# Graph network stack on one core: LSTMs over single nodes with output gates of two chunks by seven products, and GpSimd multiplying gates and writing last states

## The chip, the core and the metric

The kernel runs on one core of a Trainium2 chip. A core has five engines that run side by side, each with its own queue of instructions in a fixed order: TensorE for matrix products (PE in the profile, its weight loads PEld), VectorE (DVE), ScalarE (ACT), GpSimd (POOL) and SyncE (SP), which here issues the transfers. They wait for one another by semaphores. Matrix products land in PSUM, in banks of 512 float32 values in each of 128 partitions; the other data lie in SBUF.

The metric is the device time of one execution in microseconds (us), lower is better. Three runs of the kernel before took 2249.4, 2252.04 and 2255.14 us, median 2252.04. What a measurement of this kernel can tell from no change is about 0.3%, some 6.8 us.

## What is computed

The input is x[128, 64, 256], 128 graphs of 64 nodes with 256 features, and one adjacency matrix. Four layers run one after the other, each as `x = x + layer(relu(layernorm(x)))`. The change lies in the third, `_L2_gnn_ref`, cut here to its second half:

```python
for p in range(1, MAX_SKIP + 1):          # p = 1..4
    nw = Tv // p                          # 64 // p windows of p nodes
    wins = h[:, :nw * p, :].reshape(Bv * nw, p, Hd)
    last = _lstm_last(Wih[p - 1], Whh[p - 1], bih[p - 1], bhh[p - 1], wins)
    idx = jnp.arange(nw) * p + (p - 1)
    h = h.at[:, idx, :].set(last.reshape(Bv, nw, Hd))
# one LSTM step, state (h, c), zero at the start
g = x_t @ Wih.T + h @ Whh.T + bias
i, f, gg, o = jnp.split(g, 4, axis=-1)
c = sigmoid(f) * c + sigmoid(i) * tanh(gg)
h = sigmoid(o) * tanh(c)
```

For p = 1 a window is a single node. There is one step from a zero state, so the forget gate and Whh drop out: `h = sigmoid(o) * tanh(sigmoid(i) * tanh(g))`.

## The kernel before

All work is in float32. The 128 graphs are held as four groups q of 32 graphs, in four large tiles `big`; `nodes(q)` gives a group as H[128 partitions, 2 feature halves, 64 nodes, 32 graphs]. Sixteen tiles X0 to X15 of [128, 4, 256] hold x itself. In layer 2 each of them is written out to a buffer in device memory (`xs<-X` in the profile), after which its place serves the LSTM as scratch: `flat[i]` is X(i) seen as [128, 1024].

`windows` runs p = 1 to 4. For p = 1 there are 16 chunks of 16 nodes (four per group), worked in eight pairs; a chunk has 16 x 32 = 512 columns. `lstm(p, t, ch, Ws)` does one step of one chunk. A gate has 256 outputs, two blocks of 128. A plain product of a gate needs four matmuls of 512 columns: two output blocks by two feature halves. The kernel mostly uses a scheme of seven products of half the width (Strassen's, in the variant with few additions): the 32 graphs are cut in two halves of 16, and sums of data quarters are multiplied with sums of weight quarters.

- The data sums T0 to T3 are the four parts of a tile `ls_tx` (pool of two buffers). VectorE makes them per chunk with three subtractions: one of 128x512 (T0 and T1 together), then two of 128x256 (T2, then T3). Both inputs of these lie in SBUF.
- The weight sums S1 to S4 are made once per p by `weights(p)`, which also loads the weights: even p into tiles `ls_w`, odd p into X4 to X7 (Wih) and X0 to X3 (Whh). It is called for p + 1 before the second pair of p; SyncE and VectorE have the transfers and sums in their fixed order.
- `product(m, bank, first)` issues product m for two gates at once, each into one half of a bank. The order is 1, 6, 7, 5, 2, 4, 3, into four banks a, b, f and d; products 2, 4 and 3 add on top of banks a, f and d.
- ScalarE copies product 1 to Z (`ls_z`). VectorE adds: Z = Z + product 6; U = Z + product 7; V11 = U + product 5; V10 = Z + (7 + 4); V01 = Z + (5 + 3). The sum of products 1 and 2 is read from its bank. So product 2 has to wait for the copy of Z, product 4 for the addition U and product 3 for the addition V11, because they write into the bank that is read there.
- ScalarE applies sigmoid or tanh with the bias, quarter by quarter.

For p = 1 a chunk calls `gates` twice. The first call makes the input gate i and the candidate g, 14 matmuls of 256 columns. The second makes the output gate o on its own, by plain products, 4 matmuls of 512 columns; the results come out of PSUM by two ACTIVATEs with no addition. VectorE then multiplies i and g to c (128x1024, `X<-ls_g`), ScalarE takes tanh of c, and VectorE writes the last state into H with two multiplications of 128x512 (`last_state`, `big<-ls_g` in the profile). A float32 matmul is recorded as two MATMULs.

The order on each engine is fixed when the kernel is built, by a scheduler that follows the order of the calls and its own costs. In the profile nearly every instruction has line 799, since a helper records them all, so groups are told apart by the names of their tiles.

Of the kernel before, what the change touches and what calls it, by code (L numbers as in the profile page):

```python
# [8 lines left out]
F32 = mybir.dt.float32  # L9
# [903 lines left out]
class Fast:  # L913
# [28 lines left out]
    def act(self, out, a, f, **kw):  # L942
        return self.nc.scalar.activation(out, a, f, **kw)
# [500 lines left out]
P = 128  # L1444
NB = 16
# [20 lines left out]
class Kernel:  # L1466
# [35 lines left out]
    def begin(self):  # L1502
        nc, o, io = self.nc, self.o, self.io
        self.ident = self.c("ident", P, P)
        make_identity(nc, self.ident)
        self.ones = self.c("ones", P, P)
        nc.vector.memset(self.ones[:], 1.0)
        self.A, self.AT = self.c("A", N, N), self.c("AT", N, N)
        nc.sync.dma_start(self.A[:], io["adj"])
        nc.sync.dma_start(self.AT[:], io["adj_t"])  # L1510
        self.X = []
        for i in range(NB):
            self.X.append(self.c(f"X{i}", P, TPB, D))
        self.load_x(0)

    def load_x(self, i):
# [687 lines left out]
    def windows(self):  # L2204

        nc, o, io = self.nc, self.o, self.io
        cx, (w, wq, gp, tp, zp, psum, pst) = self.stage([("lsw", 1), ("lswq", 1), ("lsg", 2), ("lst", 2), ("lsz", 2),  # L2210
                                                         ("lsps", 7), ("lstps", 1)], "tile")
        with cx:
            bias = w.tile([P, 4, 8], F32, name="ls_b")
            bh = w.tile([P, 4, 8], F32, name="ls_bh")
            with nc.allow_non_contiguous_dma("a few values"):
                nc.sync.dma_start(bias[:], io["L2_gnn_bih"].rearrange("q (k p) -> p q k", p=P))
                nc.sync.dma_start(bh[:], io["L2_gnn_bhh"].rearrange("q (k p) -> p q k", p=P))
            o.add(bias[:], bias[:], bh[:])
            flat = [x[:].rearrange("p t d -> p (t d)") for x in self.X]
            self.c_, self.h_, self.th_ = Ring(flat[12:15]), Ring(flat[8:10]), Ring(flat[10:12])  # L2220
            self.u_ = Ring([flat[15][:, 0:512], flat[15][:, 512:1024]])
            self.lp = gp, tp, zp, psum, bias

            def load(ap, n, x):

                if x is None:
                    return ([wq.tile([P, 4 * D], F32, name=f"ls_w{n}{kc}")[:] for kc in range(2)]
                            + [wq.tile([P, 2 * D], F32, name=f"ls_s{n}{i}")[:] for i in range(3)])
                return [flat[x], flat[x + 1], flat[x + 2][:, 0:512], flat[x + 2][:, 512:1024], flat[x + 3][:, 0:512],
                        flat[x + 3][:, 512:1024]]  # L2230

            def weights(p):

                out = []
                for n, m in enumerate(("Wih", "Whh") if p > 1 else ("Wih",)):
                    t = load(None, n, None if p % 2 == 0 else 4 - 4 * n)
                    ap = io[f"L2_gnn_{m}_t"][p - 1]
                    for kc in range(2):
                        nc.sync.dma_start(t[kc], ap[kc * P:(kc + 1) * P, :])
                    A = [[t[kc].rearrange("p (x k m) -> p x k m", k=2, m=P)[:, :, k, :] for kc in range(2)]  # L2240
                         for k in range(2)]
                    S1, S2, S4 = (y.rearrange("p (x m) -> p x m", m=P) for y in t[2:5])
                    o.add(S1, A[1][0], A[1][1])
                    o.sub(S2, S1, A[0][0])
                    o.sub(S4, A[0][1], S2)
                    S3 = t[5].rearrange("p (x m) -> p x m", m=P) if len(t) > 5 else A[1][0]
                    o.sub(S3, A[0][0], A[1][0])
                    out.append({1: A[0][0], 2: A[0][1], 3: S4, 4: A[1][1], 5: S1, 6: S2, 7: S3,
                                "A": A})
                return out  # L2250

            ready = weights(1)
            for p in range(1, 5):
                Ws = ready
                nw = N // p
                parts = -(-nw // 16)
                chunks = []
                for q in range(NG):
                    w0 = 0
                    for k in range(parts):  # L2260
                        w1 = w0 + (nw - w0) // (parts - k)
                        chunks.append((q, w0, w1))
                        w0 = w1
                for n in range(0, len(chunks), 2):
                    if n == 2 and p < 4:
                        ready = weights(p + 1)
                    if n == 2 and p == 4:
                        self.fetch(0, 8)
                        for i in range(8):
                            self.back(i, pst, "pt")  # L2270
                    two = [dict(q=q, w0=w0, w1=w1) for q, w0, w1 in chunks[n:n + 2]]
                    two[-1]["last"] = p == 4 and n + 2 >= len(chunks)
                    for t in range(p):
                        for ch in two:
                            self.lstm(p, t, ch, Ws)
            self.fetch(8, NB)
# [17 lines left out]
    def lstm(self, p, t, ch, Ws):  # L2294
# [25 lines left out]

        def gates(xs, fs):
            G = gp.tile([P, 2, 1024], F32, name="ls_g")
            if p == 1 and len(xs) == 1:
                for k in range(2):
                    ps = psum.tile([P, BT], F32, name="ps")
                    for kc in range(2):
                        self.mm(ps[:, 0:2 * W].rearrange("p (w b) -> p w b", b=32), Ws[0]["A"][k][kc][:, xs[0], :],
                                node(kc), kc == 0, kc == 1)
                    self.act(G[:, 0, 2 * W * k:2 * W * (k + 1)].rearrange("p (h w b) -> p h w b", h=2, b=16),
                             ps[:, 0:2 * W].rearrange("p (w h b) -> p h w b", h=2, b=16), fs[0],  # L2330
                             bias=bias[:, p - 1, 2 * xs[0] + k:2 * xs[0] + k + 1])
                return G
            n = len(xs)
            V = G[:, 0:n, 0:4 * W].rearrange("p x (k h w) -> p x k h w", k=2, h=2)
            banks = {}

            def product(m, bank, first):
                if first:
                    banks[bank] = psum.tile([P, 2, 256], F32, name="ps")
                for i, x in enumerate(xs):  # L2340
                    for j, (A, Bm) in enumerate(parts):
                        out = banks[bank][:, i, 0:W]
                        if len(Bm[m].shape) == 3:
# [24 lines left out]
            return G  # L2368
# [24 lines left out]
        else:  # L2393
            self.last_state(H, at, W, s(G, 0), s(G, 1))

    def last_state(self, H, at, W, *factors):

        for k in range(2):
            y = H[:, k, at, :].rearrange("p w (h b) -> p h w b", h=2)
            self.o.mul(y, *(x[:, 2 * W * k:2 * W * (k + 1)].rearrange("p (h w b) -> p h w b", h=2, b=16) for x in factors))  # L2400

# [470 lines left out]
```

## Time and profile before

| what | value |
|---|---|
| median of three runs | 2252.04 us (2249.4 to 2255.14) |
| profiled execution, its time | 2254.63 us |
| its span in the profile | 2252.8 us |
| granted TensorE clock, mean | 0.997 |
| p = 1 (677.6 to 830.1 us): PE / DVE / ACT / POOL busy | 151.65 / 118.26 / 92.90 / 0.00 us of 152.5 |
| p = 2 and a part of 3 (830.1 to 1005 us): PE / DVE / ACT busy | 174.90 / 121.99 / 78.29 us of 174.9 |

Groups within p = 1, from the groups of instructions by shape in that stretch (count, mean of one): ACT ls_z copies of 128x512 x16, 600 ns; DVE additions of 128x512 from PSUM x80, 682 to 687 ns; DVE products c of 128x1024 x15, 1226 ns; DVE last states of 128x512 x30, 688 ns; ACT tanh of 128x1024 x15, 1050 ns.

A span is what the profiler saw of one execution; 2254.63 - 2252.8 = 1.83 us lie around it. Times in the trace count from the start of the span. A line of the timeline gives the start, the time from the first start to the last end of a run of like instructions, the engine, the operation, output <- inputs, shapes and count; in brackets stands how long the engine was idle before and who ended that.

### The profile page before, as it was taken

What the parts mean: (1) busy time and instruction counts of PE and PEld (TensorE: products, weight loads), DVE (VectorE), ACT (ScalarE), POOL (GpSimd) and SP (SyncE); (2) the same over time, 40 slices, a digit from 0 to 9 for tenths busy, and PEclk for the clock granted to TensorE, in tenths of its full rate; (3) what the DMA queues carried; (4) which work ended last, traced back from release to release, by engine and by line L of the source; (5) the groups of instructions that cost most, each with busy time, mean ns of one, the idle gap of its engine ahead of it and who ended that gap; (6) DMA issues with size and microseconds to landing.
All of it is one profiled execution on the core that took longest, in us unless ns stands there. A gap on an engine that the chain in (4) does not pass through costs nothing.

```text
span 2252.8 us, 33666 instructions
## 1 busy us (share of the span) xinstructions
PE 2214.0 (98%) x12617; PEld 1614.5 (72%) x12617; DVE 1610.7 (71%) x4073; ACT 1143.7 (51%) x2500; POOL 7.2 (0%) x33
## 2 busy tenths in 40 slices
PE   7999998999999999999999999999999999999999
PEld 4554444667777778888999999888888555555654
DVE  8777576888538776676767676756955787777767
ACT  5667864665435663444444443433634664444431
POOL 1000000000000000000000000000000000000000
PEclk9999999999999999999999999999999999999999
DMA  6000220122000000000100001000001000000001
GB/s 181 1 1 10 75 54 27 59 93 47 1 24 5 1 19 1 1 1 1 38 1 1 1 1 60 16 1 1 13 1 51 29 1 15 15 20 20 15 24 48
DMA packets 61070, 54.88 MB, mean 24 GB/s; under 512 B 15203, under 2 KB 58724, under 8 KB 60900
## 3 DMA queue, kind: packets, MB, share of 16 engines
q1 hardware_dynamic: 60900, 52.66, 7.6%
q8 instruction: 101, 1.65, 0.3%
q14 instruction: 69, 0.57, 0.1%
HBM read 35.86 MB, written 16.78 MB: 23 GB/s over the span
## 4 chain that ended last, share of the span: by engine, by line
PE 77%; DVE 4%; ACT 1%; issue 1%; DMA 0%; ACTq 0%; DVEq 0%
PE ps L799 70%; PE pt L799 4%; PE acc L799 3%; DVE sm_m L799 1%; DVE X L799 1%; PE pe L799 1%; DVE aw L799 1%; DVE XV L799 0%; ACT ls_g L799 0%; ACT h L799 0%; DMA ls_w<-in_L_gnn_Wih_t_dram 0%; DVE lin_s L799 0%; DVE lin_p L799 0%; DVE hT L799 0%; DVE n_st L799 0%
## 5 line engine op out<-in xcount | busy, mean ns | idle before, releaser
L799 ACT ACTIVATE ls_g<-ls_g,ls_b 128x512 f32<-128x512 f32 (+4 forms) x472 | 243.3, 565 | 146.8 <-DVE ls_g L799 144.7
L799 ACT ACTIVATE ls_g<-ps,ls_b 128x256 f32<-128x256 f32 (+3 forms) x268 | 115.6, 470 | 335.9 <-PE ps L799 332.8
L799 PE MATMUL ps<-z,w 128*128 128x512 f32 x512 | 257.1, 624 | 0.0
L799 PE MATMUL ps<-big,X 128*128 128x176 f32 (+3 forms) x848 | 212.7, 366 | 0.1
L799 DVE TENSOR_TENSOR ls_g<-ls_z,ps 128x512 f32<-128x512 f32 (+5 forms) x258 | 147.3, 577 | 90.7 <-PE ps L799 89.0
L799 PE MATMUL ps<-ls_tx,X 128*128 128x160 f32 (+2 forms) x960 | 206.9, 326 | 1.4 <-DVE ls_tx L799 0.9
L799 PE MATMUL ps<-X,X 128*128 128x160 f32 (+1 forms) x896 | 199.1, 306 | 0.0
L799 PE MATMUL ps<-X,ls_w 128*128 128x256 f32 x640 | 190.5, 379 | 0.1
L799 PEld LDWEIGHTS ps<-ls_tx,X 128*128 128x128 f32 x960 | 161.7, 190 | 16.3 <-DVE X L799 4.7
L799 DVE TENSOR_TENSOR aw<-at,ed_OST 128x1024 f32<-128x1024 f32 x128 | 150.3, 1220 | 28.7 <-PE ps L799 28.5
L799 ACT ACTIVATE r<-ps 128x512 f32<-128x512 f32 x256 | 129.4, 621 | 74.6 <-PE ps L799 74.5
L799 PEld LDWEIGHTS ps<-big,X 128*128 128x128 f32 x848 | 145.9, 190 | 29.7 <-issue 19.4
L799 DVE TENSOR_TENSOR X<-ls_g 128x1024 f32<-128x1024 f32 (+2 forms) x108 | 117.5, 1088 | 50.6 <-ACT ls_g L799 50.6
L799 PEld LDWEIGHTS ps<-X,X 128*128 128x128 f32 x896 | 148.4, 190 | 0.0
L799 PE MATMUL ps<-X,ls_s 128*128 128x256 f32 x480 | 142.7, 379 | 0.0
L799 PEld LDWEIGHTS ps<-z,w 128*128 128x128 f32 x512 | 87.5, 191 | 67.6 <-issue 60.4
L799 PE MATMUL ps<-ls_tx,ls_s 128*128 128x256 f32 x464 | 134.7, 379 | 0.0
L799 PEld LDWEIGHTS ps<-X,ls_w 128*128 128x128 f32 x640 | 121.3, 190 | 16.8 <-DVE X L799 0.5
L799 PE MATMUL ps<-ls_tx,ls_w 128*128 128x256 f32 x464 | 133.3, 380 | 0.0
L799 PE MATMUL ps<-big,ls_w 128*128 128x256 f32 x464 | 131.9, 379 | 0.7 <-ACT ls_z L799 0.7
L799 PE MATMUL ps<-aw,ed_ODT 128*32 128x512 f32 x1024 | 122.0, 593 | 0.1
L799 PE MATMUL ps<-ed_S,Q 64*128 64x512 f32 x512 | 121.0, 604 | 0.9 <-DVE X L799 0.9
(560 smaller groups left out, 3938.7 us busy)
## 6 DMA issues: line engine op xcount, KB each, us to landing
X<-in_x_dram SPq DMA_DIRECT2D x32, 512.0 KB
xs<-X SPq DMA_DIRECT2D x16, 512.0 KB
X<-xs SPq DMA_DIRECT2D x16, 512.0 KB
out_dram<-X SPq DMA_DIRECT2D x31, 256.0 KB
X<-in_L_gnn_Wih_t_dram SPq DMA_DIRECT2D x4, 512.0 KB
ls_w<-in_L_gnn_Wih_t_dram SPq DMA_DIRECT2D x4, 512.0 KB
ls_w<-in_L_gnn_Whh_t_dram SPq DMA_DIRECT2D x4, 512.0 KB
w<-in_L_gnn_W_t_dram SPq DMA_DIRECT2D x2, 512.0 KB
```

The source lines that it names most:

```text
L799: i = method(*a, **kw)
```

## The change

1. X0 to X15 become eight tiles of two, `X2`, so that two neighbours are one tile of [128, 2, 1024]. Each X is a view of half a tile.
2. For p = 1 a new function `single` replaces `lstm`, for a pair of chunks A and B at a time. It calls `gates` three times: i and g of A; i and g of B; then o of A and o of B together. Each call has seven products of two, 14 matmuls of 256 columns. The plain product is gone.
3. The gates land in a ring of five tiles, X2 numbers 4, 5, 6, 0, 1, in place of the pool `ls_g`. c is written over the gate i, and its tanh over the gate g.
4. The product c (128x1024) and the last states (two of 128x512 per chunk) are issued on GpSimd.
5. The data sums of both chunks are held until the output gates of the pair are done, in the same two buffers of `ls_tx`.

```diff
+        self.X2 = [self.c(f"X{i}", P, 2, TPB, D) for i in range(0, NB, 2)]
+        self.X = [x[:, i] for x in self.X2 for i in range(2)]
...
+            self.g_ = Ring([self.X2[i][:].rearrange("p x t d -> p x (t d)") for i in (4, 5, 6, 0, 1)])
...
                     two[-1]["last"] = p == 4 and n + 2 >= len(chunks)
+                    if p == 1:
+                        self.single(two, Ws[0])
+                        continue
...
         def gates(xs, fs):
             G = gp.tile([P, 2, 1024], F32, name="ls_g")
-            if p == 1 and len(xs) == 1:
-                for k in range(2):
-                    ps = psum.tile([P, BT], F32, name="ps")
-                    for kc in range(2):
-                        self.mm(ps[:, 0:2 * W].rearrange("p (w b) -> p w b", b=32), Ws[0]["A"][k][kc][:, xs[0], :],
-                                node(kc), kc == 0, kc == 1)
-                    self.act(G[:, 0, 2 * W * k:2 * W * (k + 1)].rearrange("p (h w b) -> p h w b", h=2, b=16),
-                             ps[:, 0:2 * W].rearrange("p (w h b) -> p h w b", h=2, b=16), fs[0],
-                             bias=bias[:, p - 1, 2 * xs[0] + k:2 * xs[0] + k + 1])
-                return G
...
+    def single(self, two, A):
+        nc, o = self.nc, self.o
+        gp, tp, zp, psum, bias = self.lp
+        I, F, G, O = range(4)
+        data = []
+        for ch in two:
+            H, at = self.nodes(ch["q"]), slice(ch["w0"], ch["w1"])
+            T = tp.tile([P, 4, 256], F32, name="ls_tx")[:].rearrange("p n (w b) -> p n w b", b=16)
+            o.sub(T[:, 0:2], H[:, :, at, 16:32], H[:, 0, at, :].rearrange("p w (h b) -> p h w b", h=2))
+            o.sub(T[:, 2], H[:, 1, at, 16:32], T[:, 0])
+            o.sub(T[:, 3], H[:, 1, at, 0:16], T[:, 2])
+            data.append({1: H[:, 0, at, 0:16], 2: H[:, 1, at, 0:16], 3: H[:, 1, at, 16:32],
+                         5: T[:, 0], 7: T[:, 1], 6: T[:, 2], 4: T[:, 3]})
+        def gates(pairs, act):
+            tile = self.g_.next()
+            V = tile.rearrange("p x (k h w) -> p x k h w", k=2, h=2)
...
+            a = product(1, "a", True)
+            self.act(Z, a, AF.Copy)
+            o.add(Z, Z, product(6, "b", True))
+            o.add(U, Z, product(7, "f", True))
+            o.add(V[:, :, 1, 1], U, product(5, "d", True))
+            a = product(2, "a", False)
+            act(V[:, :, 0, 0], a, 0)
+            o.add(V[:, :, 1, 0], Z, product(4, "f", False))
+            act(V[:, :, 1], V[:, :, 1], 1)
+            o.add(V[:, :, 0, 1], Z, product(3, "d", False))
+            act(V[:, :, 0, 1], V[:, :, 0, 1], 0)
+            return tile
...
+        def together(out, a, k):
+            self.act(out, a, AF.Sigmoid, bias=bias[:, 0, 2 * O + k:2 * O + k + 1])
+        cells = []
+        for b in data:
+            V = gates(((I, b), (G, b)), apart)
+            nc.gpsimd.tensor_tensor(V[:, 0], V[:, 0], V[:, 1], op=ALU.mult)
+            self.act(V[:, 1], V[:, 0], AF.Tanh)
+            cells.append(V)
+        V = gates([(O, b) for b in data], together)
+        for i, ch in enumerate(two):
+            self.last_state(self.nodes(ch["q"]), slice(ch["w0"], ch["w1"]), 256, V[:, i], cells[i][:, 1], engine=nc.gpsimd)
```

`apart` issues one ACTIVATE per gate (sigmoid for i, tanh for g), `together` one for both chunks. `last_state` takes the engine as an argument, VectorE where none is given.

More of the change, by code (lines that the diff above doesn't have):

```diff
@@ L1510, in begin @@
         nc.sync.dma_start(self.AT[:], io["adj_t"])
-        self.X = []
-        for i in range(NB):
-            self.X.append(self.c(f"X{i}", P, TPB, D))
+        self.X2 = [self.c(f"X{i}", P, 2, TPB, D) for i in range(0, NB, 2)]
+        self.X = [x[:, i] for x in self.X2 for i in range(2)]
         self.load_x(0)
@@ L2218, in windows @@
             o.add(bias[:], bias[:], bh[:])
-            flat = [x[:].rearrange("p t d -> p (t d)") for x in self.X]
+            flat = [x.rearrange("p t d -> p (t d)") for x in self.X]
+            self.g_ = Ring([self.X2[i][:].rearrange("p x t d -> p x (t d)") for i in (4, 5, 6, 0, 1)])
             self.c_, self.h_, self.th_ = Ring(flat[12:15]), Ring(flat[8:10]), Ring(flat[10:12])
@@ L2247, in weights @@
                     o.sub(S3, A[0][0], A[1][0])
-                    out.append({1: A[0][0], 2: A[0][1], 3: S4, 4: A[1][1], 5: S1, 6: S2, 7: S3,
-                                "A": A})
+                    out.append({1: A[0][0], 2: A[0][1], 3: S4, 4: A[1][1], 5: S1, 6: S2, 7: S3})
                 return out
@@ L2394, in lstm, with product, apart @@
             self.last_state(H, at, W, s(G, 0), s(G, 1))
-    def last_state(self, H, at, W, *factors):
+    def single(self, two, A):
[14 more added lines that the diff above has]
+            V = tile.rearrange("p x (k h w) -> p x k h w", k=2, h=2)
+            banks = {}
+            def product(m, bank, first):
+                if first:
+                    banks[bank] = psum.tile([P, 2, 256], F32, name="ps")
+                for i, (x, b) in enumerate(pairs):
+                    nc.tensor.matmul(banks[bank][:, i, :].rearrange("p (w b) -> p w b", b=16), A[m][:, x, :], b[m],
+                                     start=first and i == 0, stop=i == 1, skip_group_check=True)
+                return banks[bank][:]
+            Z = zp.tile([P, 2, 256], F32, name="ls_z")[:]
+            U = self.u_.next().rearrange("p (x w) -> p x w", x=2)
+            a = product(1, "a", True)
[10 more added lines that the diff above has]
+            return tile
+        def apart(out, a, k):
+            for i, (x, f) in enumerate(((I, AF.Sigmoid), (G, AF.Tanh))):
+                self.act(out[:, i], a[:, i], f, bias=bias[:, 0, 2 * x + k:2 * x + k + 1])
+        def together(out, a, k):
[9 more added lines that the diff above has]
+            self.last_state(self.nodes(ch["q"]), slice(ch["w0"], ch["w1"]), 256, V[:, i], cells[i][:, 1], engine=nc.gpsimd)
@@ L2398, in last_state @@
+    def last_state(self, H, at, W, *factors, engine=None):
         for k in range(2):
             y = H[:, k, at, :].rearrange("p w (h b) -> p h w b", h=2)
-            self.o.mul(y, *(x[:, 2 * W * k:2 * W * (k + 1)].rearrange("p (h w b) -> p h w b", h=2, b=16) for x in factors))
+            (engine or self.nc.vector).tensor_tensor(y, *(x[:, 2 * W * k:2 * W * (k + 1)].rearrange("p (h w b) -> p h w b", h=2, b=16) for x in factors), op=ALU.mult)
     def edges(self, w, pool, psum):
```

## The prediction

> **What bounds the kernel now.** First the page's busy times: TensorE is busy nearly always, VectorE three quarters of the time, GpSimd practically never.
>
> ```profile
> span 2252.8 us, 33666 instructions
> PE 2214.0 (98%) x12617; PEld 1614.5 (72%) x12617; DVE 1610.7 (71%) x4073; ACT 1143.7 (51%) x2500; POOL 7.2 (0%) x33
> ```
>
> A busy PE need not be the limit, so I read the chain of waits from 677 to 835 us, the stage that is changed. From the first data sums on it is TensorE alone:
>
> ```profile
> 677.85 1.64 DVE ls_tx L799 x3
> 679.53 155.48 PE ps L799 x592
> ```
>
> The busy times by stretch say the same: 151.65 us of matmuls in 152.50. Whatever makes TensorE wait here costs its full length.
>
> ```profile
> 677.60:830.10 152.50, 151.65 (x577) 109.13 (x577) 118.26 (x187) 92.90 (x160) 0.00 (x0) 1.00 0.00 1
> ```
>
> The timeline gives the pace. The same step of two neighbouring chunks:
>
> ```profile
> 727.15 2.75 PE L799 MATMUL ps<-ls_tx,X 128*128 128x256 f32 x12
> 736.63 2.75 PE L799 MATMUL ps<-ls_tx,X 128*128 128x256 f32 x12
> ```
>
> A chunk takes 736.63 - 727.15 = 9.48 us. It holds 14 matmuls of 256 columns and 4 of 512, 22 units of 256, so a unit costs 9.48 / 22 = 0.431 us. A product for two gates (two units) is 0.862 us.
>
> Two things that the change brings hardly occur before, and the timeline shows one trace of each. GpSimd, at the start of the program, beside VectorE:
>
> ```profile
> 40.20 1.49 POOL L1807 TENSOR_SCALAR big<-big 128x512 f32<-128x512 f32 x1
> 40.22 0.66 DVE L799 SCALAR_TENSOR_TENSOR f_x<-f_v,f_uk,f_x 64x57 f32<-64x57 f32 x1
> 41.77 1.26 POOL L1808 TENSOR_TENSOR big<-big 128x512 f32<-128x512 f32 x1
> 41.98 1.06 DVE L799 SCALAR_TENSOR_TENSOR f_h_t<-f_h_r,f_x,f_h_s 64x1 f32<-64x1 f32 x1
> ```
>
> and the same VectorE instruction a little earlier, alone:
>
> ```profile
> 37.58 0.21 DVE L799 SCALAR_TENSOR_TENSOR f_h_t<-f_h_r,f_x,f_h_s 64x1 f32<-64x1 f32 x1
> ```
>
> GpSimd needs 1.26 us for 128x512. An instruction of VectorE that reads two operands from SBUF stood still meanwhile, 1.06 us in place of 0.21, until 43.04, just when GpSimd was done (43.03). And the weights: Whh of p = 3 was loaded long ahead, Wih at the end of p = 1:
>
> ```profile
> 500.13 0.35 SPq L2239 DMA_DIRECT2D X<-in_L_gnn_Whh_t_dram  x1
> 829.87 1.19 SPq L2239 DMA_DIRECT2D X<-in_L_gnn_Wih_t_dram  x2
> 835.26 0.69 DVE L799 TENSOR_TENSOR X<-X,X 128x512 f32<-128x512 f32 x1 [0.20 <-DMA X<-in_L_gnn_Wih_t_dram]
> ```
>
> Two loads of 512 KB take 835.26 - 829.87 = 5.4 us from issue until a sum can use them.
>
> **The change, part by part.**
>
> *Products.* A pair had 44 units and has 42: 8 pairs x 2 x 0.431 = **-6.9 us**. That is all that can be gained, since TensorE has only some 0.85 us of idle time in the stage.
>
> *ScalarE and VectorE.* Per pair the second gate call needs a Z copy (0.60) more and five VectorE additions (back to back 0.60 each, as 732.53, 733.13, 733.73 in the trace). VectorE loses two products c (1.23) and four last states (0.65). Per pair of 18.1 us it has 15 additions and the data sums 2 x (0.60 + 0.36 + 0.36): 11.6 us. The sums of busy times fit; the order in the queues decides.
>
> *GpSimd.* Six multiplications per pair: two of 128x1024, four of 128x512 with strided output. The row says 1.26 for 512; for 1024 I take 2.45, a little under twice 1.26 (2.52). Low bound: VectorE's own 1.23 and 0.65. High bound: the longest row of that size, 1.49, and as no row writes strided, 0.3 more, as much as lies between 1.26 and 1.49 and a little: 1.8. I take the row of the same operation. Sum 4.9 + 5.04 = 9.9 us, room enough, but ScalarE's tanh of c waits in its queue for the first two, and behind it the sigmoids and the next Z copy.
>
> *A steady pair.* I set the queues in the order of the built kernel side by side by hand, with the spacings of the rows (VectorE 0.60 and 0.36; ScalarE 0.42, 0.62, 1.05; 0.20 after a matmul, as the ls_z copy; 0.05 after others). Time 0 is product 1 of chunk A.
>
> - The data sums of A may only be made when the previous output call has finished product 4, as both buffers are held. T2 of A is ready at 0.90, product 6's turn is 0.86: stall 0.09.
> - The output gates' ACTIVATEs end at 2.32; GpSimd's four last states run from 2.46 on.
> - VectorE's T2 of B comes at 2.51 and waits for the first one, to 3.72; ends 4.08. Addition Z to 4.68. T3 of B waits for the second (4.08 to 5.34), ends 5.70. Addition U, queued behind, ends 6.30. Product 4's turn is 4.39, but it overwrites what U reads: it starts at 6.35. Stall 1.96.
> - In the output call ScalarE is late: tanh of A (to 13.88, since c comes at 12.73), six gate ACTIVATEs to 16.84, Z copy to 17.42, additions Z and U to 18.72; product 4's turn is 18.41. Stall 0.36.
>
> Together 42 x 0.431 + 0.09 + 1.96 + 0.36 = 20.5 us per pair against 18.95. The first pair has no seam behind it, 19.2. Stage: 19.2 + 7 x 20.5 = 162.7 against 152.5: **+10.2 us**. If the sums need not wait for GpSimd the same table gives 18.7 per pair, 150.1, -2.4 us.
>
> *Weight sums of p = 2.* Eight sums of two SBUF inputs fall into the first two pairs, beside the first products c. One or none behind a multiplication: 0 to 2.45; I take **+1**.
>
> *The end of p = 1.* The ring's last tile, for the output gates of pair 8, is X0 and X1, the place of Whh for p = 3. So its two loads, moved from 500 us to behind GpSimd's last state, and VectorE's sum on them stands in the queue in front of addition U of the second gate call of p = 2. Counted from the start of p = 2: T2 late, product 6 +0.85. T2 of the second chunk, a sum on Wih, T3 and another sum wait for the four last states (to 8.98): product 4 +3.2, product 3 +1.0. Whh lands at 8.98 + 5.3 = 14.3; sum and U end 15.24: product 4 of the second call +2.05, product 3 behind the late product c +1.08, the next call +0.7. Together **+8.9**; 7.6 if VectorE never waits for GpSimd, 5 with the cheapest GpSimd. Before, that sum's data lay there, and the cover was all of layer 2.
>
> *Rest.* Pairing the tiles changes no order outside these stretches but two places in layer 2 where the Whh sums stood: nothing.
>
> Sum: 10.2 + 1 + 8.9 = +20.1. On the profiled 2254.63 (span 2252.8 and 1.83 around it) that is 2274.7; that run is 2.6 above the median, so 2252.04 + 20.1 = **2272 us**.
>
> Two rules of the Trainium skill may be held against this. "SBUF — State Buffer", Who interferes with whom, says that a VectorE instruction with two SBUF inputs and a GpSimd instruction that reads SBUF exclude each other for the whole instruction. The 1.06 us row agrees, but the row at 40.22 was let through after 0.4 us while GpSimd ran on for 0.8. By the rule the sum stands; with waits of 0.4 us in place of whole ones U ends a microsecond earlier, 19.5 per pair, and the sum is about +12. "GPSIMD Engine Reference", Elementwise — side-by-side cycle accounting, gives 4497 ns for 2048 float32 elements; scaled, as an estimate, 2.25 for 1024 and 1.12 for 512, with which the sum would be +15.5. Neither turns the sign.
>
> **The rivals.**
>
> 1. *No exclusion (2257 us).* GpSimd and VectorE work side by side; -2.4 in the stage, +7.6 at its end, +5.2, within no change. For it: the row at 40.22. Against it: 41.98.
> 2. *GpSimd keeps the port (2297 us).* Its four last states don't wait for one another, so VectorE may not get in between and waits for all 5 us: 23.6 per pair by the same table, stage 184.5 (+32), end +12, sum +45. In the trace the GpSimd instructions had gaps of 0.1 us between them, so it can't be seen.
> 3. *Strided last states at 1.8 us (2282 us).* Stage 170.2 (+17.7), end +11, +1: +30. For it: the one-input row of 1.49; against it: 1.26.
> 4. *Faster (2245 us).* GpSimd's work and the Whh loads are both covered; only -6.9 is left. It decides if product 4 finds U done in every call, which needs T3 of B to end by 3.7 after the seam and Whh to land by 7.2 (product 4's turn in the second call, 6.03 + 5 x 0.431 = 8.2, less 0.6 for the sum and 0.36 for U). The seam's row speaks against it.
>
> That the products don't go away is excluded: the built kernel has 42 matmuls of 256 columns per pair and none of 512.
>
> **How the numbers follow.** Forecast 0.52, rival 1 0.17, rival 2 0.13, rival 3 0.15, rival 4 0.03. A measurement of this kernel can tell about 0.3%, 6.8 us. Faster is rival 4, 0.03; same is rival 1 but for its costlier part, 0.14; slower the rest, 0.83. The range goes from the lower part of rival 1, 2255, to rival 2's 2297, and leaves out rival 4, the cheapest of rival 1 and half of rival 2.
>
> **What would show it.** Right: periods of some 20.5 us between product 1 of neighbouring pairs; TensorE idle before product 4 of chunk A, released by `X<-ls_z`; `ls_tx` subtractions of 128x256 with a mean of well over 0.42; POOL multiplications near 1.26 and 2.45; a VectorE sum at the start of p = 2 waiting for DMA `X<-in_L_gnn_Whh_t_dram` some 14 us after p = 1, and a gap of TensorE there. Wrong: periods under 18.95, subtractions of unchanged length, or no wait for Whh.

## The result, and the profile after

| | before | changed kernel |
|---|---|---|
| median | 2252.50 us (6 runs, 2249.4 to 2255.14) | 2267.81 us (6 runs, 2264.63 to 2270.38) |
| profiled execution; its span | 2254.63; 2252.8 | 2264.63; 2262.4 |
| p = 1: first data sum to first matmul with p = 2's weights | 677.85 to 830.53: 152.68 | 672.75 to 833.14: 160.39 |
| from there to the last group of matmuls with `ls_w` (p = 4) | to 1741.68: 911.15 | to 1750.93: 917.79 |

The changed kernel is slower: ratio 1.007, interval 1.006 to 1.008, +15.3 us between the medians. Layer 2 begins its windows at 672 to 678 us in the profiles of this study, for reasons that lie ahead of the change. So I compare lengths counted from the first data sum: p = 1 grew by 7.7 us and what follows by 6.6, together 14.35; that is the result within what runs differ by.

The busy times of the page. TensorE is busy 6 us less (the products that went), GpSimd 83.5 us more, VectorE about the same, and the span is longer:

```profile
span 2262.4 us, 33928 instructions
...
PE 2208.0 (98%) x12713; PEld 1629.0 (72%) x12713; DVE 1614.1 (71%) x4065; ACT 1144.2 (51%) x2500; POOL 90.7 (4%) x81
```

The stretches show where TensorE stands still (columns: stretch, its length, then busy time and instructions of PE, PEld, DVE, ACT and POOL, granted clock, share of DMA, GB/s). The four are p = 1, the first 10 us of p = 2, the 4 us after them, and then on:

```profile
672.60:833.10 160.50, 149.46 (x673) 125.19 (x673) 118.17 (x176) 93.70 (x161) 77.56 (x44) 1.00 0.01 4
833.10:842.90 9.80, 5.70 (x25) 4.41 (x25) 9.80 (x13) 3.39 (x6) 5.83 (x4) 1.00 0.38 116
842.90:846.80 3.90, 3.90 (x12) 3.09 (x12) 2.54 (x6) 2.15 (x5) 0.00 (x0) 0.56 0.31 111
846.80:1009.00 162.20, 162.20 (x751) 141.97 (x750) 114.58 (x187) 71.77 (x133) 0.00 (x0) 1.00 0.00 1
```

Before, TensorE was busy 151.65 of 152.50 us. Now TensorE is recorded idle for 11.0 us in p = 1 and for 4.1 in the first 9.8 us of p = 2. In the third row it is busy all the time, but at a granted clock of 0.56: it does in 3.9 us what takes 2.2 at full clock. After that it is never idle again in the stretch shown.

The chain of waits, where it was one single line of TensorE before (155.48 us), is now broken in each pair. Start, length, and who was at work:

```profile
735.34 0.95 DVE ls_tx L799 x2
...
736.35 1.26 issue
737.61 0.68 DVE ls_z L799
...
738.35 0.67 issue
739.02 0.69 DVE X L799
...
739.75 12.40 PE ps L799 x56
```

TensorE's 12.40 us begin only when addition U (739.02) is done, and in front of it on VectorE lie two stretches of "issue", 1.26 and 0.67 us, in which VectorE waits for nothing that the profile shows. The timeline of the same seam says what they are (start, time from first start to last end, engine, operation, shapes, count):

```profile
735.59 0.69 DVE L799 TENSOR_TENSOR ls_tx<-big 128x512 f32<-128x512 f32 x1
735.72 5.73 POOL L2454 TENSOR_TENSOR big<-X,X 128x512 f32<-128x512 f32 x4 [3.25 <-ACT X L799]
...
736.31 1.38 DVE L799 TENSOR_TENSOR ls_tx<-big,ls_tx 128x256 f32<-128x256 f32 x1
...
738.21 0.89 DVE L799 TENSOR_TENSOR ls_tx<-big,ls_tx 128x256 f32<-128x256 f32 x1
...
739.02 0.67 DVE L799 TENSOR_TENSOR X<-ls_z,ps 128x512 f32<-128x512 f32 x1
...
739.75 1.13 PE L799 MATMUL ps<-ls_tx,X 128*128 128x256 f32 x4 [1.06 <-DVE X L799]
...
754.03 0.42 DVE L799 TENSOR_TENSOR ls_tx<-big,ls_tx 128x256 f32<-128x256 f32 x1
```

The T2 subtraction of chunk B takes 1.38 us and T3 0.89, beside GpSimd's four last states; the same instruction takes 0.42 when GpSimd is idle (754.03). The additions that read PSUM stay at 0.67 to 0.69 us even beside GpSimd (739.02). TensorE then waits before product 4 of chunk A, 1.06 us by the record, 1.23 counted from the place that the last four matmuls' pace gives (737.66 + 0.86 = 738.52 to 739.75). The period from pair to pair is (818.97 - 719.69) / 5 = 19.86 us, where 42 matmul units need 18.1.

### The profile page after: what moved, and what is told of

Its sections match the earlier page's. It is cut to its first block, busy times and chain, and to the rows that moved or that the text cites. A ratio compares the mean times of both kernels' runs of the same rounds, so it can differ in the third digit from the quotient of the medians.

```text
span 2262.4 us, 33928 instructions
## 1 busy us (share of the span) xinstructions
PE 2208.0 (98%) x12713; PEld 1629.0 (72%) x12713; DVE 1614.1 (71%) x4065; ACT 1144.2 (51%) x2500; POOL 90.7 (4%) x81
## 4 chain that ended last, share of the span: by engine, by line
PE 74%; DVE 6%; issue 2%; ACT 1%; POOL 0%; DMA 0%; ACTq 0%; DVEq 0%; POOLq 0%; SPq 0%
PE ps L799 67%; PE pt L799 4%; PE acc L799 3%; DVE X L799 2%; DVE sm_m L799 1%; DVE ls_tx L799 1%; DVE aw L799 1%; PE pe L799 1%; ACT X L799 1%; DVE XV L799 0%; DVE ls_z L799 0%; POOL X L2443 0%; ACT ls_g L799 0%; ACT h L799 0%; ACT big L799 0%
## 5 line engine op out<-in xcount | busy, mean ns | idle before, releaser
L799 ACT ACTIVATE ls_g<-ls_g,ls_b 128x512 f32<-128x512 f32 (+5 forms) x408 | 208.1, 559 | 124.7 <-DVE ls_g L799 122.7
L799 PE MATMUL ps<-ls_tx,X 128*128 128x256 f32 (+2 forms) x1088 | 239.2, 334 | 11.6 <-DVE X L799 10.1
L799 ACT ACTIVATE ls_g<-ps,ls_b 128x256 f32<-128x256 f32 (+2 forms) x204 | 80.5, 438 | 305.8 <-PE ps L799 304.6
L799 PEld LDWEIGHTS ps<-ls_tx,X 128*128 128x128 f32 x1088 | 184.2, 190 | 29.7 <-DVE X L799 17.8
L799 DVE TENSOR_TENSOR ls_g<-ls_z,ps 128x512 f32<-128x512 f32 (+3 forms) x226 | 125.6, 561 | 78.1 <-PE ps L799 76.5
L799 PE MATMUL ps<-big,X 128*128 128x256 f32 (+2 forms) x816 | 181.1, 332 | 0.1
L799 PEld LDWEIGHTS ps<-big,X 128*128 128x128 f32 x816 | 139.4, 190 | 8.8 <-DVE ls_g L799 0.4
L799 DVE TENSOR_TENSOR X<-ls_z,ps 128x512 f32<-128x512 f32 (+4 forms) x185 | 112.7, 610 | 37.7 <-PE ps L799 34.8
L799 DVE TENSOR_TENSOR X<-ls_g 128x1024 f32<-128x1024 f32 (+2 forms) x92 | 97.9, 1064 | 38.9 <-ACT ls_g L799 38.9
```

What stands on the lines that cost most here:

```text
L799: i = method(*a, **kw)
```

## The experiments

Eleven kernels were run. The two lengths are those of the table above, from the first data sum; medians and ratios are of timed runs against the kernel before, measured beside them. A steady pair is the mean of the pairs behind the first ones, of one profile.

| run | median us | ratio, interval | p = 1 | after p = 1 | steady pair |
|---|---|---|---|---|---|
| kernel before | 2252.50 | | 152.68 | 911.15 | 18.95 |
| changed kernel | 2267.81 | 1.007, 1.006 to 1.008 | 160.39 | 917.79 | 19.86 |
| e1 without last states | 2253.92 | 1.0005, 0.9995 to 1.0014 | 151.37 | 913.29 | 18.44 (one of 18.74) |
| e2 last states on VectorE | 2262.27 | 1.0045, 1.0028 to 1.0062 | 161.69 | 914.71 | 19.96 |
| e3 c on VectorE | 2267.25 | 1.0067, 1.005 to 1.0083 | 158.73 | 917.23 | 19.63 (two kinds of pair in turn) |
| e4 tanh later | 2266.09 | 1.0055, 1.0038 to 1.0072 | 159.37 | 916.23 | 19.71 |
| e5 sums ahead | 2265.53 | 1.0061, 1.0044 to 1.0078 | 163.49 | 915.57 | 18.45 |
| e6 sums ahead, tanh later | 2266.75 | 1.0056, 1.0034 to 1.0077 | 162.48 | 915.39 | 18.24 |
| e7 place of Whh | 2271.90 | 1.0093, 1.0076 to 1.011 | 168.74 | 917.22 | 19.85 |
| e8 copies for last states | 2257.87 | 1.0021, 1.0011 to 1.003 | 155.86 | 913.76 | 19.00 |
| e9 nothing on GpSimd | 2260.07 | 1.0039, 1.0026 to 1.0052 | 157.98 | 915.74 | 19.75 |
| e10 everything placed | 2247.85 | 0.9979, 0.997 to 0.9988 | 149.29 | 911.53 | 18.24 (18.7 with weight sums) |
| e11 as e10, tanh first | 2249.58 | 0.9988, 0.9979 to 0.9997 | 150.84 | 911.53 | 18.46 (18.95) |

**e1: what the last states cost.**

```diff
-            self.last_state(..., V[:, i], cells[i][:, 1], engine=nc.gpsimd)
```

> The four last states per pair are left out (GpSimd only makes the products c), so the nodes keep their values through p = 1; VectorE, ScalarE and TensorE keep all their instructions. Theory A (the last states hold the T2 and T3 subtractions up, and with them addition U and product 4 of chunk A): the 128x256 subtractions fall back to 0.42 us, TensorE's stall of 1.1 to 1.5 us before product 4 of A goes, the pair falls from 19.9 to some 18.6 us (7 x 1.3 = -9), and the start of p = 2 loses the collisions too (-5): 2254 us, 2250 to 2258. Rival B (the stall comes from buffers that are held until product 4 of the output gates, whatever GpSimd does): period within 0.2 us of 19.9, time above 2264.

Measured 2253.92 us, 13.9 less than the changed kernel. The groups of the tile `ls_tx` between 700 and 815 us (count; least, median and greatest ns):

```profile
L799 DVE TENSOR_TENSOR ls_tx<-big,ls_tx x28: 410/419/425, 699.8 to 814.0; 128x256 f32<-128x256 f32 x28
L799 DVE TENSOR_TENSOR ls_tx<-big x13: 677/685/693, 701.1 to 812.3; 128x512 f32<-128x512 f32 x13
```

No subtraction is long any more, the pair takes 18.44 us and p = 2 starts 4.5 us faster. Theory A holds: nearly the whole loss hangs on the last states. What it doesn't say is whether their being on GpSimd, or their being there at all, is the matter.

**e2 and e3: the two kinds of product, each back on VectorE.**

```diff
 e2
-            self.last_state(..., cells[i][:, 1], engine=nc.gpsimd)
+            self.last_state(..., cells[i][:, 1])
 e3
-            nc.gpsimd.tensor_tensor(V[:, 0], V[:, 0], V[:, 1], op=ALU.mult)
+            o.mul(V[:, 0], V[:, 0], V[:, 1])
```

> Last states on VectorE again, c stays on GpSimd. The scheduler puts the four of them in VectorE's queue ahead of the data sums of chunk B. Theory A (queue order counts as much as the collision): four times 0.60 us wait for the output gates and stand ahead of T0/T1 of B and of addition U; product 4 of A then waits some 2.4 us instead of 1.3; period 21.0, 7 x 1.1 = +8 over the changed kernel; the start of p = 2 loses collisions, -3: 2273 us. Rival B (only the collision with GpSimd costs): 18.6 per pair, 2256 us or less.

> Products c on VectorE again, last states stay on GpSimd. Theory A (c on GpSimd is the better place in the steady pair, since VectorE is in front of the next call's additions): c of 1.15 us stands in front of addition Z of the next call, period 20.4 instead of 19.9 (+0.5 x 7 = +3.5), less the weight sums that met c in the first pairs (-1.9): 2269 us. Rival B (GpSimd's 2.36 us instead of 1.23 is what makes ScalarE late): -0.5 per pair, 2262 us.

e2, the timeline of a seam and of the output call behind it:

```profile
735.97 2.51 DVE L799 TENSOR_TENSOR big<-X,X 128x512 f32<-128x512 f32 x4
...
740.16 1.97 PE L799 MATMUL ps<-ls_tx,X 128*128 128x256 f32 x8 [0.26 <-DVE ls_tx L799]
740.53 0.42 DVE L799 TENSOR_TENSOR ls_tx<-big,ls_tx 128x256 f32<-128x256 f32 x1
...
752.66 1.13 PE L799 MATMUL ps<-ls_tx,X 128*128 128x256 f32 x4 [0.38 <-DVE X L799]
```

The collision is gone (0.42 again), but the four last states stand in VectorE's queue for 2.51 us, TensorE waits for a data sum behind them (740.16), and the output call waits for its additions (752.66): 19.96 us, no better than 19.86. At the start of p = 2 it gains 3.1. The total of 2262.27 lies between the two theories (by the two lengths of the table it is 1.8 us better than the changed kernel, the rest lies ahead of p = 1): A is right that the queue costs as much as the collision, and overstated it by a microsecond a pair. e3 fits neither: the pair takes 19.63 on average, so c is not dearer on VectorE, as A had it, and the pair is 0.23 us shorter, not the 0.5 of B; as a whole it is level with the changed kernel.

**e4: ScalarE's order.**

```diff
             act(V[:, :, 0, 0], a, 0)
+            if c is not None:
+                nc.scalar.hold = nc.scalar.last
+                self.act(c[:, 1], c[:, 0], AF.Tanh)
+                nc.scalar.hold = nc.scalar.last
...
-            self.act(V[:, 1], V[:, 0], AF.Tanh)
```

> Only the order of ScalarE is changed: tanh of c is queued behind the next call's first gate ACTIVATEs (those of product 2) instead of ahead of them. Theory A (ScalarE stands behind GpSimd's product c; that costs some 0.3 us in the output call, and the seam is limited by the subtractions): period 19.9 to 19.7, stall in the output call 0.3 to 0.7 gone but the seam's stall grows by part of it, since ScalarE's output gates come out earlier or later by as much: -1 to -2 in all, 2266 us. Rival B (the late ScalarE sets the whole pair): -0.7 per pair and more, 2261 us.

The first line, kept, issues the next call's first gate ACTIVATEs; tanh of c now follows them. 2266.09 us, a pair of 19.71: theory A. As long as the seam is late, ScalarE's lateness is worth 0.15 us a pair.

**e5 and e6: the data sums moved away from the last states.** T0 to T3 of the next pair go into the two `ls_g` buffers; a fixed order (`hold`) puts those of chunk A behind V01 of the first call and those of chunk B behind V01 of the second.

```diff
+            if after:
+                if i == 0:
+                    self.ts_ = gp.tile([P, 2, 1024], F32, name="ls_g")
+                nc.hold((None, nc.mark()[1], None))
+                ahead.append(self.node_sums(after[i], i))
+                nc.hold((None, nc.mark()[1], None))
```

> The data sums of the next pair are made half a pair earlier, between the gate calls, while GpSimd is idle; they lie in the two ls_g buffers, so four chunks have room, and the first data sums of p = 2 move ahead too. GpSimd keeps c and the last states. Theory A (with the collision away, the next wait in line appears: ScalarE behind GpSimd's product c, since the new place of the sums leaves VectorE less slack there; from the queues set side by side the pair takes 19.8): p = 1 gains only 2 us, the start of p = 2 gains 4.5 (as without last states): 2261 us. Rival B (the collision is the only wait): 18.6 per pair, -9 - 4.5: 2254 us.

> As e5_sums_ahead, and tanh of c is queued on ScalarE behind the next call's first gate ACTIVATEs, as in e4_tanh_later. Theory A (two waits, of which either alone hides the other: taken away together both go): the pair takes 18.2 us, the bound of 42 products being 18.1; p = 1 gains 12.4, the start of p = 2 another 4.5: 2251 us, level with the kernel before or just under it. Rival B (the order of ScalarE is worth no more than the 1.7 us of e4): 2259 us.

Both totals missed: 2265.53 and 2266.75. But the steady pair did come down to 18.45 and 18.24 us, near e5's rival B (18.6) and e6's theory A (18.2), and no stall over 0.2 us is left between 741 us and the end of p = 1. The time was lost in the first three pairs, and the timeline of e6 shows by what:

```profile
701.73 4.94 POOL L2469 TENSOR_TENSOR big<-X,X 128x512 f32<-128x512 f32 x4 [2.69 <-ACT X L799]
...
706.71 0.69 DVE L799 TENSOR_TENSOR ls_tx<-big 128x512 f32<-128x512 f32 x1 [3.70 <-POOL big L2469]
...
711.14 0.69 DVE L799 TENSOR_TENSOR ls_z<-ls_z,ps 128x512 f32<-128x512 f32 x1 [0.22 <-ACT ls_z L799]
...
711.16 1.24 PE L799 MATMUL ps<-big,X 128*128 128x256 f32 x4 [2.85 <-ACT ls_z L799]
...
730.00 0.69 DVE L799 TENSOR_TENSOR ls_tx<-big 128x512 f32<-128x512 f32 x1 [3.29 <-POOL big L2469]
...
731.34 1.13 PE L799 MATMUL ps<-ls_g,X 128*128 128x256 f32 x4 [3.18 <-DVE X L799]
```

As `ls_tx` had become free, the scheduler moved the first data sums of p = 2 into p = 1, behind the last states of the nodes that they read. VectorE waits 3.70 and 3.29 us for GpSimd there, with everything that is queued behind, and TensorE 2.85 and 3.18. Besides, three data sums of the next pair met a product c in these first pairs (2.57, 2.56 and 2.60 us from 686.72, 717.85 and 735.95, in place of 0.42), and TensorE waits 1.82, 1.51 and 0.60 us behind them. My edit had moved more than I meant. The last four of the eight pairs showed what the places are worth, so the next version keeps them (e10). At the start of p = 2, no longer late, e6 also shows VectorE waiting 1.16 and 1.07 us for the Whh loads, and TensorE 1.92.

**e7: the place of Whh.** Only the order of the ring is changed, so that Whh's place is free earlier.

```diff
-            self.g_ = Ring([... for i in (4, 5, 6, 0, 1)])
+            self.g_ = Ring([... for i in (1, 4, 5, 6, 0)])
```

> Only the order of the five ring tiles is changed, so that X0 to X3, the place of Whh for p = 3, are free one or two pairs before the end of p = 1; their loads no longer wait for GpSimd's last states. Theory A (the prediction's step: VectorE waits for these loads, 2.05 + 1.08 + 0.7 = 3.8): 2264 us. Rival B (the first gate call of p = 2 is so late by GpSimd's last states that the loads are there in time; the profile shows no wait on them): no change, 2267 to 2269 us.

Slower than both theories, 2271.90, all of it in p = 1 (168.74). The timeline of the last pair (SPq is the issue of a transfer):

```profile
821.20 0.33 SPq L2239 DMA_DIRECT2D X<-in_L_gnn_Whh_t_dram  x1
...
824.88 0.69 DVE L799 TENSOR_TENSOR X<-X 128x512 f32<-128x512 f32 x1 [3.64 <-DMA X<-in_L_gnn_Whh_t_dram]
...
830.78 2.08 PE L799 MATMUL ps<-ls_tx,X 128*128 128x256 f32 x4 [5.07 <-DVE X L799]
```

With its place free, the scheduler set VectorE's sums on Whh in the middle of the pair, 3.7 us after the load was issued; VectorE waits 3.64 us for the data, then stands beside a product c, and TensorE waits 5.07. So a wait on these loads is real where their sum is queued close behind them. In the changed kernel it is not there; this doesn't test what the move costs in the prediction's place, it shows only that moving them by the ring makes it worse.

**e8: a GpSimd instruction with one input.**

```diff
+            if engine:
+                engine.tensor_copy(y, factors[0][:, 2 * W * k:2 * W * (k + 1)].rearrange("p (h w b) -> p h w b", h=2, b=16))
+                continue
             (engine or self.nc.vector).tensor_tensor(y, ...
```

> The four last states on GpSimd become copies of the output gate: one input in place of two, the same strided output; the multiplication by tanh of c is left out. All queues keep their order. Theory A (whatever GpSimd reads or writes in SBUF holds a VectorE subtraction with two SBUF inputs up): the 128x256 subtractions of chunk B still take 0.9 to 1.4 us, period 19.5 to 19.9, 2262 to 2268 us. Rival B (only an instruction of GpSimd with two inputs does): the subtractions take 0.42 us, the pair 18.7 as without last states, 2254 us.

```profile
737.75 3.09 POOL L2455 COPY big<-X 128x512 f32<-128x512 f32 x4 [2.94 <-ACT X L799]
...
738.35 0.71 DVE L799 TENSOR_TENSOR ls_tx<-big,ls_tx 128x256 f32<-128x256 f32 x1
...
739.58 0.78 DVE L799 TENSOR_TENSOR ls_tx<-big,ls_tx 128x256 f32<-128x256 f32 x1
```

The subtractions take 0.71 and 0.78 us, 0.3 and 0.36 more than alone, where the multiplications had added 0.96 and 0.47; the pair takes 19.00. The pair and the median of 2257.87 lie between the two theories. Theory A holds in kind: one input is enough to hold VectorE up. But a copy of 128x512 takes GpSimd only 0.8 us (four in 3.09), and holds VectorE for less.

**e9: the scheme without GpSimd** (the edits of e2 and e3 together).

> The seven products for the output gates alone: products c and last states stay on VectorE, nothing runs on GpSimd. Theory A (GpSimd was needed, because VectorE's queue is the next limit): per pair VectorE has 11.6 + 2 x 1.23 + 4 x 0.65 = 16.7 us of 18.1, and c and the last states wait in its queue for ScalarE, in front of additions; the pair takes 19.9 (as e2) to 20.4 (as e3), p = 1 some 162 us, 2262 to 2267 us. Rival B (GpSimd is the whole loss, the scheme itself pays): 18.1 to 18.5 per pair, 2247 us.

2260.07 us, a pair of 19.75: near theory A, a little better in the pair and in the total than it said. The seven products do not pay by themselves either: VectorE's queue takes the place of GpSimd.

**e10 and e11: everything kept, only placed.** As e6, and the by-products put right: the first data sums of p = 2 between the calls of the last pair, the weight sums of p = 2 in twos behind the output gates of pairs 2 to 5, those of p = 3 in ones.

```diff
+            if not after:
+                nc.hold((None, nc.mark()[1], None))
+                self.first[i]["T"] = self.step_sums(2, 0, self.first[i])
+                nc.hold((None, nc.mark()[1], None))
...
+        if self.later:
+            nc.hold((None, nc.mark()[1], None))
+            for f, *a in self.later[:2]:
+                f(*a)
+            del self.later[:2]
```

> Everything of the change stays, GpSimd too; only places in the queues are changed. As e6_ahead_tanh, and what that moved by accident is put right: the first data sums of p = 2 are made between the gate calls of the last pair, not behind GpSimd's last states of the second pair; the weight sums of p = 2 follow two at a time behind the output gates of pairs 2 to 5, those of p = 3 one at a time behind the chunks of p = 2. Theory A (the loss of the changed kernel is all in who stands where when GpSimd holds VectorE up): every pair takes the 18.2 us that the last four of e6 show, p = 1 some 148 us (before 152.7), no stall and no slowed clock at the start of p = 2 (911 us from there to the last of its kind, as before): 2247 us, 2244 to 2250. Rival B (a new wait takes the place of each that is removed): 2255 us and more.

> As e10_placed, but tanh of c stands on ScalarE ahead of the next call's first gate ACTIVATEs again, as in the changed kernel. Theory A (with the collisions gone the late ScalarE is a wait of its own, as the pairs of 18.45 us in e5 against 18.24 in e6 say): +0.2 us a pair, +1.7 in all, 2249.5 us. Rival B (the places of the sums did it alone): 2248 us, no difference from e10.

2247.85 us, ratio 0.9979 with 1 outside its interval: better than both kernels, by 0.2% against the kernel before, inside theory A's range. That is less than the 0.3% that one measurement can tell; the two lengths together say the same, 1060.8 us against 1063.8. The stretches of e10 (p = 1, the first 9.8 us of p = 2, on):

```profile
676.30:825.70 149.40, 148.43 (x684) 126.92 (x683) 116.49 (x182) 94.39 (x161) 74.99 (x44) 1.00 0.02 5
825.70:835.50 9.80, 9.80 (x47) 8.52 (x47) 5.63 (x9) 6.46 (x14) 4.96 (x4) 1.00 0.48 158
835.50:1000.00 164.50, 164.50 (x761) 143.71 (x760) 116.31 (x190) 71.21 (x133) 0.00 (x0) 1.00 0.00 1
```

TensorE is recorded idle for 1.0 us in all of p = 1, with GpSimd as busy as in the changed kernel (74.99 us; it was 77.56), and not at all at the start of p = 2, at full clock. The subtractions, now on `ls_g`, are short, all 28 of them:

```profile
L799 DVE TENSOR_TENSOR ls_g<-big,ls_g x28: 424/426/426, 685.1 to 803.3; 128x256 f32<-128x256 f32 x28
L799 DVE TENSOR_TENSOR ls_g<-big x14: 683/684/686, 684.4 to 802.2; 128x512 f32<-128x512 f32 x14
```

Not every pair takes the 18.2 us of theory A: those with weight sums take 18.7 and more, and four of these sums still meet a last state (1.64 to 1.76 us in place of 0.69).

e11, with tanh back in its old place, is 1.7 us slower, what theory A said; the length of p = 1 (150.84 against 149.29) and of a pair (18.46 against 18.24) agree; the two intervals overlap, so the medians alone would not settle it. In e6 against e5 the same edit took 0.21 us from the steady pair too, but the total hid it.

## Why the prediction was right, and where its terms were not

The forecast was 2272 (range 2255 to 2297), slower at 0.83; it came out at 2267.81. The sum was +20.1, of which the profile shows 14.35. Term by term:

| term | forecast | measured | from |
|---|---|---|---|
| products that go, eight pairs | -6.9 | -6.9 | 42 units per pair, 12 matmul records of 256 columns in 2.59 us |
| stalls in a steady pair | 2.41 | 1.76 | 19.86 - 18.10 |
| weight sums of p = 2 beside c | +1 | +2.05 | 683.17 + 1.73 = 684.90 to 686.95 |
| start of p = 2 | +8.9 | +6.6 | 917.79 - 911.15 |

*The mechanism* was right: GpSimd's last states hold up the T2 and T3 subtractions of chunk B, addition U is queued behind, product 4 of chunk A waits for it. e1 shows that the loss goes with the last states, the durations (1.38 and 0.89 against 0.42) show that it is the subtractions that stand, and e8 that GpSimd's reading or writing is enough for it. The forecast without exclusion was 18.7 per pair; e1 measured 18.44.

*Its size in the seam* was too large: product 4 waits 1.23 us, not 1.96. The rule of the wait held. T2 of B ends at 737.69 and T3 at 739.10, each 0.28 us after the end of the multiplication that it ran into (737.40 and 738.81); all 17 subtractions of 128x256 that start beside GpSimd between 670 and 850 us end 0.28 us after the GpSimd instruction, and e8's, beside copies, 0.27 to 0.28. What I had wrong is when the multiplications end. Counted from product 1 of A (734.21), the first ends at 3.19 us, not at 3.72, since GpSimd starts it at 1.51 (735.72) and not at 2.46, and the second ends 1.41 us later, not 1.62. So T2 loses 0.96 and T3 0.47 us, where the forecast had waits of 1.21 and 0.66. The other stalls of a pair are a little larger than I had them (0.53 against 0.45). In all a pair is 0.65 us shorter than forecast; over seven pairs this is 4.5 of the 5.8 us that the sum was too high. The Trainium skill's page "SBUF — State Buffer", Who interferes with whom, has the two exclude each other for the whole instruction; the ends of the subtractions agree with it.

*Rival 2*, that GpSimd keeps VectorE out for all four last states, is refuted by the same line: T2 got in after the first of them. *Rival 1* fell by the durations and e1, *rival 3* by the 1.24 us that a last state takes where nothing disturbs it (e6: four in 4.94 us, shown above). *Rival 4* was not what happened, but its condition (product 4 finds U done in every call) is what e10 brought about by other places, and its 2245 is near e10's 2247.85.

*ScalarE in the output call* was forecast at 0.36 and is there, 0.12 to 0.48 us by the starts of its product 4; e4 takes away 0.15 us of the pair.

*The weight sums* cost twice what I took, within the bound of 2.45. One of them met the first product c and stood for all of it but a little:

```profile
682.19 2.36 POOL L2443 TENSOR_TENSOR X<-X 128x1024 f32<-128x1024 f32 x1 [320.03 <-ACT X L799]
682.38 2.72 DVE L799 TENSOR_TENSOR ls_s<-ls_s,ls_w 128x512 f32<-128x512 f32 x1
...
686.95 1.56 PE L799 MATMUL ps<-ls_tx,X 128*128 128x256 f32 x6 [1.90 <-DVE X L799]
```

*The start of p = 2* was too dear by 2.3, and its parts were wrong in both directions. The lines (the first row is GpSimd's four last states; SPq issues the Whh loads):

```profile
835.20 5.83 POOL L2454 TENSOR_TENSOR big<-X,X 128x512 f32<-128x512 f32 x4 [3.45 <-ACT X L799]
835.33 2.90 DVE L799 TENSOR_TENSOR ls_tx<-big,ls_tx 128x256 f32<-128x256 f32 x2
...
838.16 1.75 DVE L799 TENSOR_TENSOR X<-X 128x512 f32<-128x512 f32 x1
...
839.38 2.00 SPq L2239 DMA_DIRECT2D X<-in_L_gnn_Whh_t_dram  x2
...
841.97 1.13 PE L799 MATMUL ps<-ls_tx,ls_w 128*128 128x256 f32 x4 [3.31 <-DVE X L799]
...
842.93 0.85 PE L799 MATMUL ps<-big,ls_w 128*128 128x256 f32 x2
...
843.58 1.91 PE L799 MATMUL ps<-big,ls_s 128*128 128x256 f32 x4
...
846.79 0.69 DVE L799 TENSOR_TENSOR X<-X 128x512 f32<-128x512 f32 x1
```

T2 made product 6 late by 0.96 (forecast 0.85), and product 4 by 3.48 (forecast 3.2). The next wait in the forecast, 1.0 for product 3 of that call, is not there: its matmuls (843.58) wait for nothing. The step that failed is the one after it: the sum on Whh, at 846.79, doesn't wait for its loads, and there is no gap of TensorE. The forecast had 2.05 + 1.08 + 0.7 = 3.83 for it. I had let the loads start when GpSimd was done, 8.98 us after the start of p = 2, and land 5.3 later; the first is issued at 839.38, before GpSimd's end at 841.03 (7.89), the second at 841.06, and from 845 us on the DMA moves nothing. The call that needs the sum was late anyway, by the two stalls that I had added up just before. A wait of its own it is only when those are gone, as in e6. In its place stands something that I did not have at all: after 3.31 us of idle TensorE the granted clock is 0.50 to 0.57 from 843 to 846, and ten matmul records that take 2.16 us at full pace take 3.85: +1.7. So 0.96 + 3.48 + 1.7 and 0.2 of slower first matmuls are 6.3 of the 6.6.

The terms measured add up to -6.9 + 7 x 1.76 + 2.05 + 6.6 = 14.1 of the 14.35. Part of the closeness is luck: terms too many (3.8 and 1.0) and terms missing (1.7 and 0.2) in one place, a wait too long (4.5) in another, one too low (1.05) in a third.

## What to carry to other kernels

Moving elementwise work to an idle GpSimd is not free for VectorE: before doing it, list VectorE's instructions with two SBUF inputs, see which of them stand in front of what TensorE waits for, and give these a place in which GpSimd is idle; here the same work in the same engines went from +0.7% to -0.2% by that alone. Where several waits hide one another, judge an edit by the steady stretch in the profile and not by the total: e5 and e6 looked worthless by their medians and held most of the answer. And look at what else a freed buffer lets the scheduler move.

## What the runs showed of the hardware

**The clock can fall after a stall, and the length of the stall alone does not decide it.** TensorE idle for 2.69 us (e3), 2.85 and 3.18 (e6), 3.31 (the changed kernel) and 5.07 (e7) went on at about half the clock: 0.54 over 3.6 us in e3 and over 6.4 in e7. Idle for 1.90 us in the changed kernel (686.95) and for 1.82 in e6 it went on at 1.00. But the same wait of 1.90 us in e8 was followed by a clock of 0.52 from 690.6 to 693.6 us, and 2.72 us in e4 by 1.00 up to 852:

```profile
689.61 1.88 PE L799 MATMUL ps<-ls_tx,X 128*128 128x256 f32 x6 [1.90 <-DVE X L799]
...
845.25 1.13 PE L799 MATMUL ps<-ls_tx,ls_w 128*128 128x256 f32 x4 [2.72 <-DVE X L799]
```

The clock records of the traces show why. Within one trace the clock changes only on a grid of 3.41 us (e6: down at 712.04, up at 715.46, down at 732.52, up at 735.94), and the half clock lasts 3.41 us there, or 6.83 in e7. Between 660 and 860 us, over all the traces, the clock fell behind each of the ten pieces of this grid in which TensorE was idle for 1.90 us or more, and behind none with 1.86 or less; e4's 2.72 us lie across two pieces. The stall of 3.31 us cost 1.7 us more than its idle time, and e8's p = 1 is longer by as much for its 1.90. The Trainium skill's page "TensorE: Matmul & The Clock Gate", What's actually happening, tells of a half-rate clock after an idle window of about 3.4 us; the half and the length agree, but here 1.90 us of idle time in a piece was enough.

- **A wait for the other engine's access looks like work.** VectorE's instruction is recorded as long (1.38 for 0.42 us), no releaser is named, and the chain of waits calls it "issue". The sign is a group whose greatest duration is far above its least while nothing in its shape changed.
- **GpSimd's prices**: 1.24 us for a multiplication of 128x512 with strided output undisturbed (e6, four in 4.94), 1.46 on average beside VectorE; 2.36 for 128x1024; 0.61 for a copy of 128x512 that nothing disturbs (e8, at 739.48), 0.8 on average beside VectorE.
- **What a VectorE instruction with two SBUF inputs loses that meets one**: in the changed kernel it ends a fixed time after the GpSimd instruction, 0.28 us for 128x256 and 0.55 for 128x512, so it loses what is left of that instruction less 0.14 us: 0.96, 0.47, and 2.03 for the weight sum of 2.72.
- **The two take turns**: at the start of p = 2 GpSimd has four last states queued (835.20 to 841.03), and a VectorE instruction with two SBUF inputs gets in behind each of the first three. GpSimd waits in its turn. In the seam its first last state, begun at 735.72 while T0 and T1 of B ran to 736.28, takes 1.68 us in place of 1.24.
- **A stall costs a little more than its idle time says**, also at full clock: four matmuls right after one take 0.96 us to the next in place of 0.86 (739.75 to 740.71).
